# A feed-forward on 256 tokens at a time with its outputs turned, inside an attention kernel

## The chip, the cores and the metric

The kernel runs on one core of a Trainium2 chip. The metric is the device time of one execution in microseconds; lower is better. Besides the timed runs there is one execution taken with the hardware profiler, from which every duration below comes.

## The reference

Four sequences of 2048 tokens with 512 features go through one attention layer with 16 heads of 32 features and one linear layer with weights of +1 and -1, each followed by a residual addition and a normalization. Everything is float32. The essential part is:

```python
q = (x @ Wq.T), k = (x @ Wk.T), v = (x @ Wv.T)          # each split in 16 heads of 32
attn = softmax(q @ k.T / sqrt(32))                       # per head, over 2048 keys
x = layernorm(x + attn @ v)
w = (weights >= 0) * 2 - 1
y = clip((x @ w.T) * scale + bias, -100, 100)            # scale and bias: one per output feature
out = layernorm(x + y)
```

## The kernel before, in words

**Steps.** The attention of four heads is one group `n`, so there are 16 groups (four batch items, four groups of heads each). A group has 64 steps: four blocks of 512 queries (`qb`), each with 16 chunks of 128 keys (`kc`). The whole kernel is one sequence of 1024 steps (`total`), with a lead-in before step 0 and a tail after step 1023. The order of every engine's instructions is the order in which the Python code emits them; nothing is reordered later.

**What a step does.** `scores` (L323) subtracts a maximum (L327) and multiplies queries and keys (L333) for four heads, into four of the eight PSUM banks; ScalarE takes the exponentials (L340) into a buffer `p` from a pool with five buffers. `max_unit` (L264) computes scores for queries some 20 steps ahead (L275), into four other banks, and takes their maxima: VectorE reads three heads from PSUM (L282), and ScalarE copies the fourth to SBUF (`moved`, L294) for VectorE to reduce later. In each even step `weighted` (L344) multiplies the exponentials of the two steps before with the values (L351), and VectorE adds the result to `oT` (L363). GpSimd adds up the exponentials of each block (L377), one addition of 128 x 2048 values a step, 14 a block; two steps into the next block `denominators` (L400) multiplies these sums with ones (L383).

**What fills the odd steps.** All other work on TensorE is a task with a first and a last step, planned ahead by `plan` (L762): "small" tasks (four transposes of 128 x 128: `transpose_x` L221, `turn` L552, `add_attention` L425, weights L136 and L149) and "big" ones (a piece of a projection, L233: `project_q` and `project_k` with 256 columns and weight 2, called wide here; `project_v` with 128 columns, a value piece; and half a feed-forward tile). An odd step takes one small task and big ones of a total weight of about two. Tasks whose last step has come are taken first; the rest follow a fixed order of preference and, in a second pass, a quota of the weights over a group's 64 steps. Fillers are emitted after the step's maximum matmuls and before `later()`, the reduction of `moved`.

**PSUM banks.** `take` (L83) hands out the bank that a small clock model expects free first; eight banks are taken in each step by scores and maxima alone, and a filler takes a ninth. Who is late with a bank holds a later matmul.

**The feed-forward.** `Finish` (L481) works on 512 tokens: load the attention's result, statistics, normalize (`norm`, L542), then for each 128 tokens `turn` (L548): four transposes, a copy rounded to the one-pass float type on ScalarE (`high`, L557), and the rest `low` on VectorE (L559). `ffn` (L563) multiplies both with the weights: the tokens are the stationary operand and the weights stream, so the outputs are [token, feature]. A call covers 256 output features (`half`), or 512 in the last blocks. VectorE then multiplies by scale (L575), adds bias (L576), clips (L577), each on a tile in PSUM, and adds to the row (L579). `finish` (L611) spreads this over the next batch item's steps, one tile every 13 steps; `finish_last` (L632) and `finish_end` (L659) do it for the last batch item, at its end and in the tail. After it come second statistics, `rstd`, `shift`, `norm` and the stores, issued by SP like all loads.

The planner's choice among big tasks before the change:

```python
elif must:
    can = values[:1] or thirds[:1]
elif k == 1:
    can = values[:1] or thirds[:1] or wide[:1]
elif thirds and values:
    can = thirds[:1] + values[:1]
else:
    can = wide[:1] or values[:2] or thirds[:1]
```

Of the kernel before, what the change touches and what calls it, by code (L numbers as in the profile page):

```python
# [21 lines left out]
def kernel(  # L22
# [13 lines left out]
    P = 128  # L36
# [13 lines left out]
    STEPS = NQB * NT  # L50
    HALF = D // 2
    W = 2 * P
# [6 lines left out]
    xpool = ctx.enter_context(tc.tile_pool(name="xpool", bufs=2))  # L59
    stage = ctx.enter_context(tc.tile_pool(name="stage", bufs=2))  # L60
    mpool = ctx.enter_context(tc.tile_pool(name="mpool", bufs=2))
    cpool = ctx.enter_context(tc.tile_pool(name="cpool", bufs=1))
    dram = ctx.enter_context(tc.tile_pool(name="dram", bufs=1, space=bass.MemoryType.DRAM))
# [3 lines left out]
    vpool = ctx.enter_context(tc.tile_pool(name="vpool", bufs=2))  # L67
    ppool = ctx.enter_context(tc.tile_pool(name="ppool", bufs=5))
    apool = ctx.enter_context(tc.tile_pool(name="apool", bufs=2))
    work = ctx.enter_context(tc.tile_pool(name="work", bufs=2))  # L70
    once = ctx.enter_context(tc.tile_pool(name="once", bufs=1))
# [87 lines left out]

    scale_bc = const.tile([P, D], F32, name="scale_bc")  # L160
    bias_bc = const.tile([P, D], F32, name="bias_bc")

    def load_first():

        first = ppool.tile([P, DC, D], F32, tag="p", name="first_w")
        for i, name in enumerate(("wk", "wq", "wv")):
            xin[name, 0] = first[:, i, :]
        for name in ("wk", "wq"):
            nc.scalar.dma_start(out=xin[name, 0], in_=rows_of[name][ds(0, P), :])
        for g in range(NQB):  # L170
            t = ppool.tile([P, NTQ, D], F32, tag="p", name="first_x")
            for j in range(NTQ):
                xin[0, g, j] = t[:, j, :]
                nc.sync.dma_start(out=t[:, j, :], in_=x[0, ds(g * QB + j * P, P), :])

    def load_rest():
        nc.scalar.dma_start(out=xin["wv", 0], in_=wv[ds(0, P), :])
        raws["ws"] = xpool.tile([P, DC, D], F32, tag="xg", name="raw_ws")
        nc.scalar.dma_start(out=raws["ws"], in_=w_ffn.rearrange("(c p) i -> p c i", p=P))
        nc.sync.dma_start(out=scale_bc, in_=ffn_scale.partition_broadcast(P))  # L180
        nc.sync.dma_start(out=bias_bc, in_=ffn_bias.partition_broadcast(P))

# [295 lines left out]

    shared = []

    class Finish:  # L481
        def __init__(self, b, g):
            self.b, self.g = b, g
            self.mv, self.rs, self.nb, self.nT, self.rows_rs = {}, {}, {}, {}, {}
            self.room = None

# [61 lines left out]
        def turn(self, j):  # L548
            i = take()
            pt = cols_of(i, DC, P)  # L550
            for c in range(DC):
                nc.tensor.transpose(pt[:, c, :], self.row(j)[:, ts(c, P)], ident)  # L552
            runs("full", 0.44)

            high = work.tile([P, DC, P], F32R, tag="high", name="high")
            low = work.tile([P, DC, P], F32R, tag="low", name="low")
            nc.scalar.copy(high, pt)  # L557
            spend("ACT", 0.6, clock["PE"] + 0.2)
            nc.vector.tensor_tensor(low, pt, high, ALU.subtract)  # L559
            give(i, "DVE", 0.7)  # L560
            self.nT[j] = high, low

        def ffn(self, j, half):  # L563
            cols = slice(0, D) if half is None else ts(half, HALF)
            wide = D if half is None else HALF
            i = take()
            py = ps[:, i, :wide]
            for k, part in enumerate(self.nT[j]):
                for c in range(DC):
                    nc.tensor.matmul(  # L570
                        py, lhsT=part[:, c, :], rhs=wT["ws"][:, c, cols],
                        start=(k == c == 0), stop=(k == 1 and c == DC - 1),
                    )
            runs("full", 3.4e-3 * wide)
            nc.vector.tensor_tensor(py, py, scale_bc[:, cols], ALU.mult)  # L575
            nc.vector.tensor_tensor(py, py, bias_bc[:, cols], ALU.add)  # L576
            nc.vector.tensor_scalar(py, py, MAX_VAL, -MAX_VAL, ALU.min, ALU.max)  # L577
            dst = self.row(j)[:, cols]
            nc.vector.tensor_tensor(dst, dst, py, ALU.add)  # L579
            give(i, "DVE", 0.6 + 4.2e-3 * wide)  # L580

# [28 lines left out]

    def finish(b, qb, a, every, w, lag):  # L611
        f = Finish(b, qb)
        at(a, f.load)
        for j in range(NTQ):
            at(a + 2 + j, f.stats, 1, j)
        at(a + 6, f.rstd, 1)
        at(a + 7 + lag, f.shift, 1)
        for j in range(NTQ):
            t = a + 8 + lag + every * j
            at(t, f.norm, 1, j)  # L620
            turned = task("small", t + 1, t + 3, f.turn, j)
            for k in range(2):
                task("big", t + 2, t + w, f.ffn, j, k, after=turned)
            at(t + w, f.stats, 2, j)
        e = a + 9 + lag + every * (NTQ - 1) + w
        at(e, f.rstd, 2)
        at(e + 1 + lag, f.shift, 2)
        for j in range(NTQ):
            at(e + 2 + lag + j, f.norm, 2, j)
        at(e + 5 + lag, f.store)  # L630

    def finish_last(qb, last):  # L632
# [8 lines left out]
        at(a + 4, f.shift, 1)  # L641
        for j in range(NTQ):
            t = a + 5 + (j if late else 3 * j)
            by = t + 6
            at(t, f.norm, 1, j)
            if late:
                by = total + (-1, 1, 4, 5)[j]
            turned = task("small", t + 1, t + 3, f.turn, j)
            for k in [None] if late else range(2):
                task("big", by if late else t + 2, by, f.ffn, j, k, after=turned)  # L650
            at(by + late, f.stats, 2, j)
        e = total + 7 if late else a + 21
        at(e, f.rstd, 2)
# [5 lines left out]
    def finish_end(qb, last):  # L659
# [3 lines left out]
        for j in range(NTQ + 1):  # L663
# [3 lines left out]
            if j:  # L667
                at(total + 3, f.shift, 1, j - 1, j)
                at(total + 3, f.norm, 1, j - 1)
        for j in range(NTQ):  # L670
            t = total + (6, 6, 7, 8)[j]
            turned = task("small", t, t, f.turn, j)
            t = total + 7 + j
            task("big", t, t, f.ffn, j, None, after=turned)
            at(t, f.stats, 2, j)
            at(t, f.rstd, 2, j, j + 1)
            at(t + 1, f.shift, 2, j, j + 1)
            at(t + 1, f.norm, 2, j)
            at(t + 1, f.store_tile, j)

# [5 lines left out]
    task("small", -9, -7, transpose_weight, "wv", 0)  # L686
    for _ in range(2):
        at(-8, load_next)
# [7 lines left out]
    for n in range(N):  # L696
# [32 lines left out]
        for qb in range(NQB):  # L729
# [12 lines left out]
            if g == NG - 1:  # L742
                if b < B - 1:
                    every = 13 if b < B - 2 else 11
                    finish(b, qb, (b + 1) * NG * STEPS + qb * (5 * every - 1), every, every, 3)
                else:
                    (finish_end if is_last(n, qb) else finish_last)(qb, last)
# [7 lines left out]

    def on_vector(t):
        return t[3].__name__ == "ffn"

    def weight(t):
        return 2 if t[3] in (project_k, project_q) else 1  # L760

    def plan(quota=None):  # L762
# [9 lines left out]
        while any(len(gone[kind]) < len(tasks[kind]) for kind in tasks):  # L772
# [10 lines left out]
            for kind in most:  # L783
# [8 lines left out]
                if kind == "big":  # L792
                    if middle and quota is not None and not heavy:
                        k = max(1, min(k, -(-quota[group] * (at_n + 1) // STEPS) - used[group]))


                    thirds = [t for t in can if on_vector(t)]
                    values = [t for t in can if t[3] is project_v]
                    wide = [t for t in can if weight(t) == 2]
                    if heavy or any(map(on_vector, must)):  # L800
                        thirds = []
                    k -= sum(map(weight, must))
                    if k < 1:
                        can = []
                    elif must:
                        can = values[:1] or thirds[:1]
                    elif k == 1:
                        can = values[:1] or thirds[:1] or wide[:1]
                    elif thirds and values:
                        can = thirds[:1] + values[:1]  # L810
                    else:
                        can = wide[:1] or values[:2] or thirds[:1]
                else:
                    can = can[: max(0, k - len(must))]
                picked = must + can
                for t in sorted(picked, key=lambda t: not on_vector(t)):
                    gone[kind].add(t[2])
# [93 lines left out]
```

## Time and profile before

| what | us |
|---|---|
| median of 3 runs | 4385.39 (4384.27 to 4385.4) |
| the profiled execution, its own time | 4384.56 |
| its span | 4382.7 |
| TensorE busy, granted clock 0.996 | 4331.6 |
| GpSimd busy | 4083.0 |
| VectorE busy | 3381.3 |
| ScalarE busy | 2994.6 |

A row of the groups names the line, engine, operation, what is written and read, the shapes and the count; then the busy time of all, the mean of one in ns, and the idle time of the engine before them with what ended it. A row of the timeline has the start, the length and then the same names; PE is TensorE's matmuls, PEld its weight loads, DVE is VectorE, ACT ScalarE, POOL GpSimd. A float32 matmul stands as two instructions, as it takes two passes. A matmul that waits for a bank is listed as long, not as idle, so TensorE's busy time contains waits. A row of the waits gives the total, the number and the longest.

### The profile page before, as it was taken

The numbers are of one execution on the slowest core, as the hardware profiler recorded it, in microseconds if no ns is written. First come the engines' busy times: TensorE is split into PE (matmuls) and PEld (weight loads), VectorE is DVE, ScalarE is ACT, GpSimd is POOL, SyncE is SP. The second block draws the span as 40 slices with busy tenths as digits, with TensorE's granted clock in tenths as the row PEclk, the third lists the DMA queues.
The fourth block names the chain that finished last, engine by engine and source line by source line (L and its number), as shares of the span: only waits on it lengthen the run. The fifth ranks groups of instructions, "written<-read, shape, count | busy, mean of one in ns | idle before, by whom it ended". The sixth has DMA issues, their size and how long they took to land.

```text
span 4382.7 us, 88304 instructions
## 1 busy us (share of the span) xinstructions
PE 4331.6 (99%) x35644; PEld 2081.3 (47%) x35644; DVE 3381.3 (77%) x5924; ACT 2994.6 (68%) x6173; POOL 4083.0 (93%) x937
## 2 busy tenths in 40 slices
PE   9999999999999999999999999999999999999997
PEld 5444444444444444445444444444544444444443
DVE  6777777777778777777777877877787777878785
ACT  4666666676667667676676766767666676767675
POOL 4999999999999999999999999999999999999993
PEclk9999999999999999999999999999999999999998
DMA  2000000010001000011000100001100000001101
GB/s 74 11 14 17 11 21 10 16 40 17 21 13 29 11 23 20 11 45 36 21 20 11 33 10 21 23 10 49 28 20 21 20 21 23 20 11 33 24 23 49
DMA packets 259938, 101.60 MB, mean 23 GB/s; under 512 B 168908, under 2 KB 234444, under 8 KB 259528
## 3 DMA queue, kind: packets, MB, share of 16 engines
q1 hardware_dynamic: 258568, 94.12, 8.7%
q8 instruction: 279, 4.57, 0.4%
q10 hardware_dynamic: 960, 1.84, 0.1%
q14 instruction: 131, 1.07, 0.1%
HBM read 54.52 MB, written 33.02 MB: 20 GB/s over the span
## 4 chain that ended last, share of the span: by engine, by line
PE 94%; DVE 2%; POOL 2%; ACT 2%; issue 0%; DMA 0%; ACTq 0%; POOLq 0%; DVEq 0%; SPq 0%
PE ps L275 21%; PE ps L351 21%; PE ps L333 19%; PE ps L233 16%; PE ps L327 8%; PE ps L383 3%; PE ps L570 3%; POOL acc L377 2%; ACT p L340 1%; PE ps L425 1%; PE ps L221 1%; PE ps L552 1%; DVE part L282 1%; DVE st L516 0%; DVE ps L576 0%
## 5 line engine op out<-in xcount | busy, mean ns | idle before, releaser
L377 POOL TENSOR_TENSOR acc<-acc,p 128x2048 f32<-128x2048 f32 x825 | 3744.2, 4538 | 104.1 <-ACT p L340 43.8
L340 ACT ACTIVATE p<-ps 128x512 f32<-128x512 f32 x4096 | 2115.0, 602 | 1148.4 <-PE ps L333 1143.4
L282 DVE TENSOR_REDUCE part<-ps 128x1 f32<-128x512 f32 x3072 | 1933.4, 683 | 660.4 <-PE ps L275 659.8
L275 PE MATMUL ps<-kT,qT 32*128 32x512 f32 x8192 | 1190.5, 592 | 1.9 <-ACT p L340 1.5
L333 PE MATMUL ps<-qT,kT 32*128 32x512 f32 x8192 | 1083.6, 593 | 0.0
L351 PE MATMUL ps<-p,vv 128*32 128x512 f32 x8192 | 984.9, 598 | 1.6 <-DVE low L559 1.0
L275 PEld LDWEIGHTS ps<-kT,qT 32*128 32x128 f32 x8192 | 568.2, 184 | 429.8 <-issue 206.5
L282 DVE TENSOR_REDUCE part<-moved 128x1 f32<-128x512 f32 x1024 | 692.5, 676 | 0.3 <-ACT moved L294 0.3
L294 ACT COPY moved<-ps 128x512 f32<-128x512 f32 x1024 | 631.2, 616 | 20.4 <-PE ps L275 19.7
L351 PEld LDWEIGHTS ps<-p,vv 128*32 128x32 f32 x8192 | 220.3, 109 | 687.4 <-issue 338.4
L327 PE MATMUL ps<-negm,ones_bf 32*128 32x512 bf16 x4096 | 458.2, 384 | 11.6 <-DMA negm<-split 3.9
L333 PEld LDWEIGHTS ps<-qT,kT 32*128 32x128 f32 x8192 | 406.2, 184 | 53.5 <-issue 37.5
L363 DVE TENSOR_TENSOR oT<-ps,oT 128x512 f32<-128x512 f32 x448 | 309.8, 692 | 123.1 <-PE ps L351 81.6
L377 POOL TENSOR_TENSOR acc<-p 128x2048 f32<-128x2048 f32 x64 | 291.0, 4546 | 108.7 <-ACT p L340 108.6
L327 PEld LDWEIGHTS <-ones_bf 32*128 32x128 bf16 x4096 | 106.4, 91 | 558.2 <-issue 521.3
L233 PEld LDWEIGHTS ps<-wvT,xT 128*128 128x128 f32 x2048 | 247.7, 191 | 102.0 <-ACT p L340 96.1
L233 PE MATMUL ps<-wvT,xT 128*128 128x128 f32 x2048 | 283.2, 282 | 0.3 <-ACT p L340 0.3
L233 PE MATMUL ps<-xT,wqT 128*128 128x256 f32 x1024 | 250.6, 388 | 0.0
L233 PE MATMUL ps<-xT,wkT 128*128 128x256 f32 x1024 | 247.2, 387 | 0.2 <-ACT p L340 0.2
L233 PEld LDWEIGHTS ps<-xT,wqT 128*128 128x128 f32 x1024 | 184.1, 189 | 69.2 <-ACT p L340 48.6
L233 PEld LDWEIGHTS ps<-xT,wkT 128*128 128x128 f32 x1024 | 185.3, 190 | 61.3 <-ACT p L340 38.9
L361 DVE COPY oT<-ps 128x512 f32<-128x512 f32 x64 | 44.3, 692 | 131.4 <-PE ps L351 131.4
(76 smaller groups left out, 1755.4 us busy)
## 6 DMA issues: line engine op xcount, KB each, us to landing
xc<-in_L_attn_x_dram SPq DMA_DIRECT2D x60, 256.0 KB
res<-xc SPq DMA_DIRECT2D x60, 256.0 KB
xs<-in_L_attn_x_dram SPq DMA_DIRECT2D x48, 256.0 KB
xg<-res SPq DMA_DIRECT2D x12, 1024.0 KB
out_dram<-xg SPq DMA_DIRECT2D x12, 1024.0 KB
first_x<-in_L_attn_x_dram SPq DMA_DIRECT2D x16, 256.0 KB
xg_last<-res SPq DMA_DIRECT2D x4, 768.0 KB
out_dram<-xg_last SPq DMA_DIRECT2D x3, 1024.0 KB
```

The source lines that it names most:

```text
L233: nc.tensor.matmul(pp, lhsT=lhs(c), rhs=rhs(c), start=(c == 0), stop=(c == DC - 1))
L275: nc.tensor.matmul(ps[:, banks[h], :], lhsT=qT[n, qb][rows, ts(qc, P)], rhs=kT[n][rows, ts(kb, QB)], start=True, stop=True,)
L282: nc.vector.tensor_reduce(part[:, qc, h : h + 1, kb], src, AX.X, ALU.max, negate=True)
L294: nc.scalar.copy(moved, ps[:, banks[-1], :])
L327: nc.tensor.matmul(ps[:, banks[h], :], lhsT=ones_bf[rows, :], rhs=negm[n, qb][rows, :], start=True, stop=False,)
L333: nc.tensor.matmul(ps[:, banks[h], :], lhsT=kT[n][rows, ts(kc, P)], rhs=qT[n, qb][rows, :], start=False, stop=True,)
L340: nc.scalar.activation(p[:, h, :], ps[:, banks[h], :], AF.Exp, scale=SM_SCALE)
L351: nc.tensor.matmul(pb[cols, :], lhsT=vv[n][:, kc, cols], rhs=p[:, h, :], start=(i == 0), stop=(i == 1),)
L363: nc.vector.tensor_tensor(outs[n, qb], pb, outs[n, qb], ALU.add)
L377: nc.gpsimd.tensor_tensor(a, before if kc == 1 else a, p, ALU.add)
L383: nc.tensor.matmul(ps[h * HD : (h + 1) * HD, b, :], lhsT=ones, rhs=p[:, h, :], start=start, stop=stop,)
L570: nc.tensor.matmul(py, lhsT=part[:, c, :], rhs=wT["ws"][:, c, cols], start=(k == c == 0), stop=(k == 1 and c == DC - 1),)
```

## The change

Two tiles of 128 tokens are worked on together as a pair. `turn` writes its `high` and `low` into one half of tiles 256 tokens wide. `ffn` makes the weights the stationary operand and streams the 256 tokens, so the outputs are [feature, token]; a call covers two groups of 128 features, 16 matmuls into one bank. Because a feature is now a partition, scale and bias are one value a partition: ScalarE applies both in one activation for each 128 features, and VectorE clips both into `yT`. A new small task `turn_out` turns 128 tokens back with four transposes, and VectorE adds them to the row.

The planner gives a call of `ffn` weight 2; the former preference for feed-forward beside values is gone. The odd step takes one value piece where a small task is there (`light`) or the quota is not behind, and otherwise a wide task or two value pieces. `finish` has a pair every 26 steps, one block of 512 tokens in each group of 64 steps (22 and 54 in the third batch item). The pools change: `p` 5 to 4 buffers, `work` (`high`, `low`, new `yT`) 2 to 1, `stage` 2 to 3 with one more load in flight, `cpool` 1 to 2. The last blocks and the tail are planned anew in pairs.

```diff
-    stage = ctx.enter_context(tc.tile_pool(name="stage", bufs=2))
+    stage = ctx.enter_context(tc.tile_pool(name="stage", bufs=3))
...
-    cpool = ctx.enter_context(tc.tile_pool(name="cpool", bufs=1))
+    cpool = ctx.enter_context(tc.tile_pool(name="cpool", bufs=2))
...
-    ppool = ctx.enter_context(tc.tile_pool(name="ppool", bufs=5))
+    ppool = ctx.enter_context(tc.tile_pool(name="ppool", bufs=4))
...
-    work = ctx.enter_context(tc.tile_pool(name="work", bufs=2))
+    work = ctx.enter_context(tc.tile_pool(name="work", bufs=1))
...
-        nc.sync.dma_start(out=scale_bc, in_=ffn_scale.partition_broadcast(P))
-        nc.sync.dma_start(out=bias_bc, in_=ffn_bias.partition_broadcast(P))
+        nc.sync.dma_start(out=scale_t, in_=ffn_scale.rearrange("(c p) -> p c", p=P))
+        nc.sync.dma_start(out=bias_t, in_=ffn_bias.rearrange("(c p) -> p c", p=P))
...
-            high = work.tile([P, DC, P], F32R, tag="high", name="high")
-            low = work.tile([P, DC, P], F32R, tag="low", name="low")
+            if j % 2 == 0:
+                self.parts = [
+                    work.tile([P, DC, 2 * P], F32R, tag=part, name=part) for part in ("high", "low")
+                ]
+            high, low = (part[:, :, ts(j % 2, P)] for part in self.parts)
...
-        def ffn(self, j, half):
...
+        def ffn(self, pair, half):
+
+            if half == 0:
+                self.yT = work.tile([P, DC, 2 * P], F32, tag="yT", name="yT")
             i = take()
...
-            nc.vector.tensor_tensor(py, py, scale_bc[:, cols], ALU.mult)
-            nc.vector.tensor_tensor(py, py, bias_bc[:, cols], ALU.add)
-            nc.vector.tensor_scalar(py, py, MAX_VAL, -MAX_VAL, ALU.min, ALU.max)
-            dst = self.row(j)[:, cols]
-            nc.vector.tensor_tensor(dst, dst, py, ALU.add)
-            give(i, "DVE", 0.6 + 4.2e-3 * wide)
+            py = cols_of(i, 2, 2 * P)
+            for f in range(2):
+                for k, part in enumerate(self.parts):
+                    for c in range(DC):
+                        nc.tensor.matmul(
+                            py[:, f, :], lhsT=wT["ws"][:, c, ts(2 * half + f, P)],
+                            rhs=part[:, c, :],
+                            start=(k == c == 0), stop=(k == 1 and c == DC - 1),
+                        )
+            runs("full", 1.9)
+            for f in range(2):
+                oc = slice(2 * half + f, 2 * half + f + 1)
+                nc.scalar.activation(
+                    py[:, f, :], py[:, f, :], AF.Identity,
+                    bias=bias_t[:, oc], scale=scale_t[:, oc],
+                )
+            spend("ACT", 0.75, clock["PE"] + 0.2)
+            nc.vector.tensor_scalar(
+                self.yT[:, 2 * half : 2 * half + 2, :], py, MAX_VAL, -MAX_VAL, ALU.min, ALU.max
+            )
+            give(i, "DVE", 0.7)
+
+        def turn_out(self, j):
+
+            i = take()
+            pt = cols_of(i, DC, P)
+            for c in range(DC):
+                nc.tensor.transpose(pt[:, c, :], self.yT[:, c, ts(j % 2, P)], ident)
+            runs("full", 0.44)
+            nc.vector.tensor_tensor(self.row(j), self.row(j), ps[:, i, :], ALU.add)
+            give(i, "DVE", 0.7)
...
+    def pair(f, i, turn, ffn, back):
+
+        for k in range(2):
+            t = task("small", *turn[k], f.turn, 2 * i + k, after=halves[0])
+        for k in range(2):
+            t = task("big", *ffn[k], f.ffn, i, k, after=t)
+        halves[0] = t
+        for k in range(2):
+            task("small", *back[k], f.turn_out, 2 * i + k, after=t)
+            at(back[k][1] + 1, f.stats, 2, 2 * i + k)
...
+        for i in range(2):
+            t = a + 11 + every * i
+            at(t, f.norm, 1, 2 * i)
+            at(t + 2, f.norm, 1, 2 * i + 1)
+            z = t + every
+            pair(f, i, [(t + 1, t + 5), (t + 3, t + 7)], [(t + 4, z - 10), (t + 4, z - 8)],
+                 [(t + 6, z - 4), (t + 6, z - 2)])
...
-                    every = 13 if b < B - 2 else 11
-                    finish(b, qb, (b + 1) * NG * STEPS + qb * (5 * every - 1), every, every, 3)
+                    every, apart = (26, STEPS) if b < B - 2 else (22, 54)
+                    finish(b, qb, (b + 1) * NG * STEPS + qb * apart, every)
...
-        return 2 if t[3] in (project_k, project_q) else 1
+        return 2 if t[3] in (project_k, project_q) or t[3].__name__ == "ffn" else 1
...
+                    due = quota[group] * (at_n + 1) / STEPS - used[group] if quota else 2
...
+                    light = steps[s] and values and not heavy and due < 2.5
                     if k < 1:
                         can = []
...
+                    elif must or k == 1:
+                        can = values[:1] or ([] if must else wide[:1])
+                    elif light or due < 1.25 and not heavy:
+                        can = values[:1] or wide[:1]
                     else:
-                        can = wide[:1] or values[:2] or thirds[:1]
+                        can = wide[:1] or values[:2]
```

## The prediction

> **What bounds the kernel now.** I read the busy shares first, then the chain of work that ended last, the groups by line, the waits, and last the timeline.
>
> ```profile
> PE 4331.6 (99%) x35644; PEld 2081.3 (47%) x35644; DVE 3381.3 (77%) x5924; ACT 2994.6 (68%) x6173; POOL 4083.0 (93%) x937
> PE 94%; DVE 2%; POOL 2%; ACT 2%; issue 0%; DMA 0%; ACTq 0%; POOLq 0%; DVEq 0%; SPq 0%
> ```
>
> TensorE holds 94% of the chain, so time is what TensorE's instructions take plus the places where it waits. GpSimd is close behind: a block of 16 steps has 14 additions (L377) of 4.54 us that follow each other every 4.61 us, 64.6 us, and some blocks last 64.0 us.
>
> A busy TensorE hides its waits, because a held matmul counts as busy. So I cut the timeline at the first L327 matmul of each step and sorted the steps by the tasks the planner put into the odd one. The odd step with half a feed-forward tile (L570) and a value piece (L233) shows the method:
>
> ```profile
> 1190.04 0.40 PE L327 MATMUL ps<-negm,ones_bf 32*128 32x512 bf16 x4
> ...
> 1194.12 0.39 PE L327 MATMUL ps<-negm,ones_bf 32*128 32x512 bf16 x4
> ...
> 1195.20 1.76 PE L275 MATMUL ps<-kT,qT 32*128 32x512 f32 x8
> ...
> 1195.37 0.42 DVE L579 TENSOR_TENSOR xg<-xg,ps 128x256 f32<-128x256 f32 x1
> ...
> 1195.85 0.29 PEld L275 LDWEIGHTS ps<-kT,qT 32*128 32x128 f32 x2 [0.45 <-DVE xg L579]
> ...
> 1196.90 0.16 PEld L351 LDWEIGHTS ps<-p,vv 128*32 128x32 f32 x8 [0.76 <-ACT p L340]
> ...
> 1198.75 0.10 PEld L327 LDWEIGHTS <-ones_bf 32*128 32x128 bf16 x4 [0.84 <-issue]
> ```
>
> The odd step lasts 4.08 us and the even one 4.63, where an unheld even step lasts 3.90: the fourth head of the next maximum (L275) waits for the bank that VectorE frees after its four operations, 1.67 us into the even step. The wait is 0.73, so a bank that is free 0.94 us into the step costs nothing. The list of waits has this row 63 times:
>
> ```profile
> PEld ps L275 <- DVE xg L579: 28.3, 63, 0.5
> ```
>
> Mean length of an odd step and its even one (without denominators), same method: nothing 6.99; v (a value piece) 7.33; turn v 8.04 (the bank waits for ScalarE's `high`, then VectorE's `low`); wide (a q or k piece) 8.07; v v 8.05; x-transpose v 7.49; half alone 8.24; turn wide 8.30; half v 8.72; half wide 9.12; wide wide 9.59.
>
> **The change, part by part.** VectorE loses 112 x (423+433+433+420) ns and 8 x 2.77 us, 214 us, and gets 64 clips of 0.70 and 64 additions of 0.69, 89 us. By itself that is worth nothing, since VectorE doesn't set the end; it pays only through the banks. TensorE gets 64 x 4 transposes of 0.49 us a group (L552 to L233), 31 us; the matmuls of the feed-forward stay 32 of 256 columns a pair of tiles. ScalarE gets 128 activations.
>
> What those cost is the disputed number. The nearest rows:
>
> ```profile
> L237 ACT COPY qT<-ps 128x256 f32<-128x256 f32 x128 | 47.7, 373 | 49.8 <-PE ps L233 47.3
> L535 ACT ACTIVATE nb<-mv,neg 128x1 f32<-128x1 f32 x128 | 27.9, 284 | 1.2
> L531 ACT ACTIVATE neg<-rs 128x1 f32<-128x1 f32 x8 | 1.5, 193 | 0.2 <-POOL rs L524 0.2
> L542 ACT ACTIVATE xg<-xg,nb,rs 128x512 f32<-128x512 f32 x96 | 80.8, 841 | 0.0
> L577 DVE TENSOR_SCALAR ps<-ps 128x256 f32<-128x256 f32 x112 | 48.5, 433 | 3.9
> L577 DVE TENSOR_SCALAR ps<-ps 128x512 f32<-128x512 f32 x8 | 5.6, 700 | 0.3
> ```
>
> A plain 256-column copy takes 373 ns. But the new activation reads scale and bias from a column each. The trace has 193 ns for one column with a number as scale and 284 with a column, and 841 for 512 columns with two, against 616 for the copy L294. The Trainium skill, ScalarE: Activation LUTs, section What ACT_TABLE_LOAD costs, agrees and speaks against the change: each such operand adds about 93 ns to 186 + 0.833 a column, 585 ns here as an estimate. I take 373 + 2 x 93 = 0.56 us, ends 0.37 and 0.62.
>
> Both halves of a pair's 16 matmuls fill one bank; the built program posts once after all 16, and the second activation waits for the first. So from the next step's start: TensorE's result at +0.10 (the copy after a wide piece starts there, next rows), two activations 1.12 with 0.08 of hand-overs, the clip 0.70: bank free at +2.0.
>
> ```profile
> 1203.16 0.10 PEld L327 LDWEIGHTS <-ones_bf 32*128 32x128 bf16 x4 [0.33 <-issue]
> 1203.26 0.37 ACT L237 COPY qT<-ps 128x256 f32<-128x256 f32 x1 [0.63 <-PE ps L233]
> ```
>
> In the built program the fourth L275 head of the next step is again the one behind it: a wait of 2.0 - 0.94 = 1.06. The odd step is 0.226+0.858+0.957 for scores and maximum and 2.1 to 2.2 for 16 matmuls (16 x 0.131), 4.14. The pair lasts 4.14 + 3.90 + 1.06 = 9.10. With the copy's row it would be 8.73, with ends rounded outward 8.7 and 9.3. VectorE, held by the clip, starts its maxima late and still ends inside the step; ScalarE is through at +1.3, where its exponentials start anyway. For `turn_out` beside a value piece I take x-transpose v, 7.50 (VectorE's addition is done at +0.35), ends 7.47 and, if it behaves as turn v, 8.04; beside a wide piece 8.30.
>
> The order of both built programs, from the planner's new rule, gives the exchange in 64 steps. In six of the eleven groups with a feed-forward in the middle: gone are 6 v, 6 half v, 2 turn wide, wide wide, half wide and half: 43.98 + 52.32 + 16.60 + 9.59 + 9.12 + 8.24 = 139.9. New are 4 double halves, 4 v v, 3 wide, 2 turn v, 2 out v, 2 out wide: 36.4 + 32.2 + 24.2 + 16.1 + 15.0 + 16.6 = 140.5. So +0.6 a group. The 31 us of transposes are nearly paid by fewer held steps. With the other five by the same table: **+4**, ends -14 (8.73) and +25 (9.3 and 8.04).
>
> Four `p` buffers for five: the exponential of step s now needs the addition of step s-4. I laid additions 4.61 apart beside the steps. At five the least lead is about 1 us in steps 80 to 220, and the denominators (L383) wait 3.7 us there in total. At four the lead falls to -3.4 at worst: 5.7 us are lost on the exponentials, and the denominators' waits go. **+2**, ends 0 and +6. Later the least lead is 2.2 us, in blocks of 66 us.
>
> Steps 960 to 1023 have no projections. From 961 to 976 I get 68.3 against 66.5 (two double halves), 65.0 against 68.3 for the next 16 (three empty odd steps); from 993 to 1008, 70.1 now, GpSimd's 64.6 is the floor. That would be -7; late waits are poorly known: **-5**, ends -10 and +3.
>
> The tail, from the last attention addition (L468, 4343.8) to the end, is 38.9 us, nearly all VectorE at four operations of 0.7 a tile. In pairs, ScalarE's order sets it: last normalization at 7.5; four activations of the pair before, 9.8; `high` twice, `low`, 11.8; two halves, 15.5; activations, clip, turn, additions, 20.0; second pair's `high`, `low`, halves, 25; but the first pair's nine last ScalarE instructions stand ahead of its last two activations, 30.1; clip, turn, additions, statistics, 35.1; normalizations 40.5; store 5.5: 46. **+7**, ends +2 and +13, the upper for a TensorE clock that is 0.77 in that window already.
>
> Queues: SP issues two small loads for two broadcasts, one more `xs` load ahead and `xc` into a second buffer; stores move but follow their normalization. No such DMA stands among the waits; the `negm` transposes behind them have 5 steps of cover. Nothing, and 4 us if one came late (the longest such wait was 4.7). `high`, `low` and `yT` have one buffer; the next pair's turn is planned after the last half, so nothing in the middle; in the tail it is counted.
>
> The sum is made on the profiled execution, 4384.56 (span 4382.7): +4 +2 -5 +7 = +8, 4392.6; the median of the runs is 0.8 above it: **4393**.
>
> **Rivals.** Faster: activations at the copy's 0.37, and fewer v steps leaving less lateness to the wide ones (they range from 7.87 to 8.2). Double halves at 8.73 give -13 instead of +4, 4376, and less lateness a few us more: about 4371. For it: many fewer held steps; against it: the two-column rows.
>
> Slower, one mechanism: the bank behind the double half. If it is free at +2.5 rather than +2.0 (half alone is already held 1.15), 52 such pairs cost 26 more: 4419. The point at which it decides is +2.02, where 4394.2 is passed: very near. For it: three operations on two engines in series where a copy was one; against it: VectorE is idle when the clip comes.
>
> GpSimd as the bound through the fourth buffer: only where blocks come under 64.6 us or the lead of 2.2 us is used up; one us in each of 44 blocks would give 4437. The blocks of 66 us speak against it.
>
> **How the numbers follow.** No change can be told within 0.2%, 4376.6 to 4394.2. As summed, 0.42 (0.33 inside that band, 0.09 above it, since 4393 lies near its edge); held bank 0.26; GpSimd or a longer tail 0.10; faster 0.22, of it 0.02 inside. Together: faster 0.20, same 0.33 + 0.02, slower 0.09 + 0.26 + 0.10. Range: the sum's ends that are likely together, 4370 to 4420, leave out the GpSimd case and the deepest gain.
>
> **What would show it.** The new activations' mean (0.56), double-half pairs at 9.1, a wait of L275 on the clip about 50 times, out v at 7.5, L340 waiting for L377 only in steps 80 to 260, a tail of 46 us. Wrong would be: waits of the exponentials on L377 in every block, or activations near 0.37.

## The result and the profile after

The changed kernel takes 4414.75 us (median of 5 runs, 4414.12 to 4416.56), the kernel before beside it 4385.4 (4384.27 to 4387.53): ratio 1.0067, 95% interval 1.0056 to 1.0078. It is slower by 29 us. The prediction was 4393 with a range of 4370 to 4420: the range holds it, but the likeliest case was 22 us too low.

First the busy shares and the chain of work that ended last, of the kernel after:

```profile
PE 4345.3 (98%) x35964; PEld 2089.9 (47%) x35964; DVE 3262.4 (74%) x5572; ACT 3057.9 (69%) x6301; POOL 4083.7 (93%) x937
PE 90%; POOL 6%; DVE 2%; ACT 1%; issue 1%; DMA 0%; ACTq 0%; POOLq 0%; DVEq 0%; SPq 0%
```

VectorE lost 119 us, and the kernel is slower all the same. TensorE is listed 13.7 us busier: transposes were added, and held matmuls count as busy. GpSimd's share of the chain went from 2 to 6%; a part of it is shown further down.

The two profiled executions (4382.7 and 4412.3 us of span), cut at the same places as in the prediction, in us:

| stretch | before | after | difference | predicted |
|---|---|---|---|---|
| start to step 256 (fewer `p` buffers) | 1109.1 | 1110.8 | +1.7 | +2 |
| steps 256 to 959 (the feed-forward) | 2954.5 | 2970.8 | +16.3 | +4 |
| step 960 to the last attention addition | 280.2 | 283.5 | +3.3 | -5 |
| tail behind it | 38.9 | 47.3 | +8.4 | +7 |

So two terms were right and two were not: 12 us are missing in the middle and 8 near the end.

**The pair that the prediction worked out.** The timeline of a double half and the even step behind it, after (engine, line, instruction, tiles; in brackets the idle time before it and what ended it):

```profile
1304.58 0.39 PE L326 MATMUL ps<-negm,ones_bf 32*128 32x512 bf16 x4
...
1304.74 1.11 ACT L579 ACTIVATE ps<-ps,bias_t,scale_t 128x256 f32<-128x256 f32 x2 [0.43 <-PE ps L571]
...
1305.89 0.69 DVE L584 TENSOR_SCALAR yT<-ps 128x512 f32<-128x512 f32 x1 [1.44 <-ACT ps L579]
1305.92 2.06 ACT L339 ACTIVATE p<-ps 128x512 f32<-128x512 f32 x4
...
1306.63 0.29 PEld L274 LDWEIGHTS ps<-kT,qT 32*128 32x128 f32 x2 [0.77 <-DVE yT L584]
...
1309.54 0.40 PE L326 MATMUL ps<-negm,ones_bf 32*128 32x512 bf16 x4
```

The even step starts at 1304.58; the activations start 0.16 later, take 1.11 together, the clip ends at 1306.58. The bank is free 2.00 us into the step, and the fourth head of the maximum goes on then. The even step lasts 4.96 where an unheld one lasts 3.90: a wait of 1.06. The pair's mean over 41 is 9.11. The groups and the waits, after:

```profile
L579 ACT ACTIVATE ps<-ps,bias_t,scale_t 128x256 f32<-128x256 f32 x128 | 68.8, 538 | 33.9 <-PE ps L571 31.4
L584 DVE TENSOR_SCALAR yT<-ps 128x512 f32<-128x512 f32 x64 | 44.2, 691 | 113.8 <-ACT ps L579 113.8
L594 PE MATMUL ps<-ident,yT 128*128 128x128 f32 x256 | 43.1, 291 | 12.1 <-DVE yT L584 11.9 <-ACT p L339 0.2
```

```profile
ACT ve L519 <- DVE mv L514: 42.0, 19, 5.4
PEld ps L274 <- DVE yT L584: 38.7, 50, 0.8
ACT p L339 <- POOL acc L376: 20.4, 13, 2.5
```

The wait on the clip stands there 50 times, 0.77 us each. It takes the place of the 63 waits on the old addition. The first row is the one that I hadn't foreseen. Before, the same wait was this:

```profile
ACT ve L522 <- DVE mv L517: 26.8, 11, 6.1
```

Between steps 256 and 959 it stood there once before, with 0.9 us; now it stands there 11 times, with 2.35 to 3.34 us each.

**The wait that was missed.** The timeline after around the last statistics of a block of 512 tokens, in a step with one value piece (L513 and L514 are the statistics, L519 adds epsilon for the reciprocal deviation, `rstd`):

```profile
1646.78 0.68 DVE L513 BATCH_NORM_STATS2 st<-xg 128x6 f32<-128x512 f32 x1
1647.49 0.18 DVE L514 BATCH_NORM_AGGREGATE mv<-st 128x2 f32<-128x6 f32 x1
...
1647.71 0.30 ACT L519 ACTIVATE ve<-mv,eps_t 128x4 f32<-128x4 f32 x1 [2.36 <-DVE mv L514]
1647.91 2.04 ACT L339 ACTIVATE p<-ps 128x512 f32<-128x512 f32 x4
1648.54 0.97 PEld L232 LDWEIGHTS ps<-wvT,xT 128*128 128x128 f32 x8 [1.89 <-ACT p L339]
```

`pair` puts the statistics of the last row one step behind its `turn_out`, at z-1, and `finish` puts `rstd` at z-1 too. ScalarE reaches L519 before VectorE has done the statistics, waits 2.36 us, and its exponentials stand behind. They free TensorE's banks late: the value piece starts 1.89 us late, where an undisturbed one starts 0.76 late. Such a v pair lasts 8.51 us, not 7.33.

### The profile page after: what moved, and what is told of

Its sections match the earlier page's. It is cut to its first block, busy times and chain, and to the rows that moved or that the text cites. A ratio compares the mean times of both kernels' runs of the same rounds, so it can differ in the third digit from the quotient of the medians.

```text
span 4412.3 us, 88749 instructions
## 1 busy us (share of the span) xinstructions
PE 4345.3 (98%) x35964; PEld 2089.9 (47%) x35964; DVE 3262.4 (74%) x5572; ACT 3057.9 (69%) x6301; POOL 4083.7 (93%) x937
## 4 chain that ended last, share of the span: by engine, by line
PE 90%; POOL 6%; DVE 2%; ACT 1%; issue 1%; DMA 0%; ACTq 0%; POOLq 0%; DVEq 0%; SPq 0%
PE ps L274 21%; PE ps L350 20%; PE ps L332 18%; PE ps L232 15%; PE ps L326 7%; POOL acc L376 6%; PE ps L382 3%; PE ps L571 3%; DVE part L281 1%; ACT p L339 1%; PE ps L220 1%; PE ps L424 1%; PE ps L594 1%; PE ps L549 1%; DVE st L513 0%
## 5 line engine op out<-in xcount | busy, mean ns | idle before, releaser
L281 DVE TENSOR_REDUCE part<-ps 128x1 f32<-128x512 f32 x3072 | 1932.9, 683 | 695.8 <-PE ps L274 694.0
L332 PE MATMUL ps<-qT,kT 32*128 32x512 f32 x8192 | 1071.3, 591 | 0.0
L274 PEld LDWEIGHTS ps<-kT,qT 32*128 32x128 f32 x8192 | 553.0, 185 | 446.8 <-issue 242.4
L281 DVE TENSOR_REDUCE part<-moved 128x1 f32<-128x512 f32 x1024 | 692.4, 676 | 14.2 <-ACT moved L293 14.2
L326 PE MATMUL ps<-negm,ones_bf 32*128 32x512 bf16 x4096 | 438.8, 384 | 12.8 <-ACT p L339 4.2
```

The source lines that it names most:

```text
L274: nc.tensor.matmul(ps[:, banks[h], :], lhsT=qT[n, qb][rows, ts(qc, P)], rhs=kT[n][rows, ts(kb, QB)], start=True, stop=True,)
L281: nc.vector.tensor_reduce(part[:, qc, h : h + 1, kb], src, AX.X, ALU.max, negate=True)
L326: nc.tensor.matmul(ps[:, banks[h], :], lhsT=ones_bf[rows, :], rhs=negm[n, qb][rows, :], start=True, stop=False,)
L332: nc.tensor.matmul(ps[:, banks[h], :], lhsT=kT[n][rows, ts(kc, P)], rhs=qT[n, qb][rows, :], start=False, stop=True,)
```

## The experiments

The differences between experiments below are of medians, those of a stretch of profiled executions. All but the one on the kernel before are edits of the changed kernel.

### Reciprocal deviation later

```diff
-        at(z - 1, f.rstd, 2)
+        at(z + 1, f.rstd, 2)
```

> The changed kernel with one edit: in the middle of the kernel the second reciprocal deviations (rstd) stand two steps later, not in the step of the last statistics. Theory: ScalarE's small activation there waits 2.4 us for VectorE's statistics and holds the exponentials, 1.18 us a time, 11 or 12 times: 13 to 14 us less, 4401. Rival (that wait is hidden, and the loss lies in the bank behind the double halves alone): unchanged, 4413 to 4416.

Measured: 4404.74 (4401.05 to 4406.02), ratio to before 1.0038 (1.0023 to 1.0053), 10 us less than the changed kernel. v pairs fell from 7.89 on the mean to 7.34. In one of the groups with 22 steps a pair instead of 26, however (steps 832 to 895), 3.5 us were lost. The waits of this experiment have the reason, a row that the changed kernel has once and with 2.8 us:

```profile
ACT neg L528 <- POOL rs L521: 8.7, 3, 3.4
```

`shift` (L528) stands at z+3, two steps behind this `rstd`. The power is computed on GpSimd, where it queues between additions of 4.5 us, and two steps were too few twice. The longest of these waits, 3.4 us, is in step 881, in the group that lost; soon behind it the granted TensorE clock is 0.5 for 3.4 us. One step later instead of two should have the gain without this loss:

```diff
-        at(z - 1, f.rstd, 2)
+        at(z, f.rstd, 2)
```

> The changed kernel with the reciprocal deviation of the second normalization one step behind the last statistics, and not two as in the earlier run of this kind, which gained 10 us in all but lost 3.5 us in the group with the longer spacing. Theory (only the wait in the same step costs; the loss in that group came of the second step's delay): 11 v pairs at 7.3 instead of 8.51 are -13, none lost, so 4401 to 4402. Rival (the loss in that group is the price of any delay): 4404 to 4406. Rival (one step is not enough for VectorE to get there, so the wait stays): 4411 or above.

Measured: 4399.06 (4397.08 to 4399.81), ratio 1.0029 (1.0018 to 1.0041), 15.7 less than the changed kernel. The row of the missed wait, here:

```profile
ACT ve L519 <- DVE mv L514: 11.1, 9, 5.4
```

The group that lost 3.5 us now gains 1.1, and steps 256 to 959 take 2958.4, 12.4 less. That is +3.9 against before, where the prediction has +4. The theory stands: one line that puts two tasks into the same step is 12.4 of the 16.3 us of the middle. Another 2.2 went from the stretch behind step 960, where step 985 had the same wait (4.95 to 2.48).

### Numbers instead of columns

```diff
-                    bias=bias_t[:, oc], scale=scale_t[:, oc],
+                    scale=1.25,
```

This leaves the scale and bias of each feature out.

> The changed kernel with scale as a number (1.25) and no bias in the new activations; the real scale and bias are left out of the computation. Theory: an activation falls from 0.54 to about 0.37, the bank behind a double half is free 0.33 us sooner, the wait of 1.06 falls to 0.73 in some 46 pairs: 15 us less, 4400. Rival (the activations lie beside other work, and something else holds the step): unchanged within 3 us.

Measured: 4395.19, ratio 1.0021 (1.0013 to 1.0028), 19.6 less.

```profile
L579 ACT ACTIVATE ps<-ps 128x256 f32<-128x256 f32 x128 | 47.1, 368 | 35.0 <-PE ps L571 32.6
```

538 ns became 368, the copy's price; each column operand costs 85. The double half went from 9.11 to 8.76, by 0.35, what two activations lost (0.34): the time is on the path in full. 41 pairs by 0.35 are 14.4 of the 15.8 us that the middle lost. What of the 19.6 lies outside the middle (0.5 at the start, 1.9 behind step 960, 1.4 in the tail) wasn't followed.

### Five `p` buffers again, and four in the kernel before

```diff
-    stage = ctx.enter_context(tc.tile_pool(name="stage", bufs=3))
+    stage = ctx.enter_context(tc.tile_pool(name="stage", bufs=2))
...
-    cpool = ctx.enter_context(tc.tile_pool(name="cpool", bufs=2))
+    cpool = ctx.enter_context(tc.tile_pool(name="cpool", bufs=1))
...
-    ppool = ctx.enter_context(tc.tile_pool(name="ppool", bufs=4))
+    ppool = ctx.enter_context(tc.tile_pool(name="ppool", bufs=5))
...
-    for _ in range(3):
+    for _ in range(2):
```

> The changed kernel with five buffers for p again, and two for the x loads and one for xc as before. Theory: the fifth buffer matters only in steps 80 to 260, where waits on the exponentials are exchanged for waits of the denominators: 2 to 3 us less, 4412. Rival (GpSimd, 6% of the chain instead of 2%, is what was lost): 15 us less or more, 4400.

Measured: 4411.59, ratio 1.0055 (1.004 to 1.007), 3.2 less; the start is 1108.9, about what it was before. And the kernel before with one buffer less, its first weights laid into the pool of the sums:

```diff
-    ppool = ctx.enter_context(tc.tile_pool(name="ppool", bufs=5))
+    ppool = ctx.enter_context(tc.tile_pool(name="ppool", bufs=4))
...
-        first = ppool.tile([P, DC, D], F32, tag="p", name="first_w")
+        first = apool.tile([P, DC, D], F32, tag="acc", name="first_w")
```

> The kernel before with one edit: four buffers for p instead of five (the first weights then lie in the pool of the sums, as in the change). Theory: 2 to 3 us more, 4388, all of it in steps 64 to 260. Rival (the fourth buffer costs in every block): 15 us more or above.

Measured: 4388.0, ratio 1.0004 (0.9995 to 1.0013), so about 2 us, which its interval doesn't tell from none. Both directions, 3.2 and about 2, are near the +2 of the prediction, the second not clear of noise, and the rival of GpSimd as the bound in every block through the fourth buffer is out.

### The clip away from the bank

If the activation writes to SBUF, the bank is free 0.7 us earlier, before the clip:

```diff
-                    py[:, f, :], py[:, f, :], AF.Identity,
+                    self.yT[:, 2 * half + f, :], py[:, f, :], AF.Identity,
...
-            nc.vector.tensor_scalar(
-                self.yT[:, 2 * half : 2 * half + 2, :], py, MAX_VAL, -MAX_VAL, ALU.min, ALU.max
-            )
-            give(i, "DVE", 0.7)
+            give(i, "ACT", 1.1)
+            y = self.yT[:, 2 * half : 2 * half + 2, :]
+            nc.vector.tensor_scalar(y, y, MAX_VAL, -MAX_VAL, ALU.min, ALU.max)
+            spend("DVE", 0.7, clock["ACT"])
```

> The changed kernel with the new activations writing to yT in SBUF, and the clip done there in place, so that the bank is free after ScalarE. Theory: free at +1.3 instead of +2.0, the wait behind a double half falls from 1.06 to 0.35 in some 46 pairs: 32 us less, 4383, near the kernel before. Rival (VectorE's place in its own queue, not the bank, holds the step): the clip still stands before VectorE's maxima, so less than 8 us.

Measured: 4471.27, ratio 1.0191 (1.0176 to 1.0206), 56 us more. A miss in sign. The clip's row in this experiment:

```profile
L585 DVE TENSOR_SCALAR yT<-yT 128x512 f32<-128x512 f32 x64 | 147.5, 2305 | 117.1 <-ACT yT L579 117.1
```

The same clip takes 2305 ns instead of 691, now that it reads SBUF. The timeline of this experiment shows two clips, each with GpSimd's additions around it:

```profile
1191.91 13.84 POOL L376 TENSOR_TENSOR acc<-acc,p 128x2048 f32<-128x2048 f32 x3
...
1196.99 4.39 DVE L585 TENSOR_SCALAR yT<-yT 128x512 f32<-128x512 f32 x1 [1.28 <-ACT yT L579]
```

```profile
1321.51 4.55 POOL L376 TENSOR_TENSOR acc<-acc,p 128x2048 f32<-128x2048 f32 x1
1325.92 1.02 ACT L579 ACTIVATE yT<-ps,bias_t,scale_t 128x256 f32<-128x256 f32 x2 [3.07 <-PE ps L571]
1326.98 0.43 DVE L585 TENSOR_SCALAR yT<-yT 128x512 f32<-128x512 f32 x1 [4.04 <-ACT yT L579]
```

The second clip starts after an addition has ended (1326.06) and before the next (1333.40): 0.43 us. The first starts at 1196.99, while one of the additions runs; this one ends at 1201.09 and the clip at 1201.37, 0.28 later. So it is with all 64: the 50 clips that start while an addition runs end 0.28 to 0.29 us after that addition, and the 14 others take 0.39 to 0.43. So the clip waits for the end of the addition that runs. The Trainium skill (SBUF — State Buffer, section SBUF: two separate sides) says so: VectorE and GpSimd share a pair of ports that is locked for a whole instruction, against VectorE operations in a two-port mode or with two inputs in SBUF; and VectorE: DVE Perf Modes, section Why PSUM operands drop a tier, has a PSUM operand rule that mode out. The trace agrees with both: 0.43 alone in SBUF, and 0.66 to 0.69 from PSUM beside the same additions. Not every read of SBUF waits: the maximum of `moved` (L281, 128 x 512 from SBUF) took 0.69 at most, 1024 times in this experiment. I had carried the PSUM price over to SBUF, beside an engine that adds 93% of the time.

Two more things are in this trace. The even step behind nearly every double half is 0.88 shorter than in the changed kernel, so the bank did come free sooner. And between steps 256 and 959 the granted TensorE clock is 0.5 in nine stretches of 3.4 or 6.8 us, 51 us together, where the changed kernel has none. At half clock half of that time is lost at most, so up to 26 of the 56 us are the clock's, as an estimate; what lets it fall was not tested.

With the activation still writing to SBUF, but the clip behind the turn back, in PSUM before the addition, the lock is out of play:

```diff
-            nc.vector.tensor_tensor(self.row(j), self.row(j), ps[:, i, :], ALU.add)
-            give(i, "DVE", 0.7)
+            y = ps[:, i, :]
+            nc.vector.tensor_scalar(y, y, MAX_VAL, -MAX_VAL, ALU.min, ALU.max)
+            nc.vector.tensor_tensor(self.row(j), self.row(j), y, ALU.add)
+            give(i, "DVE", 1.4)
```

> The changed kernel; the new activations write to yT in SBUF, and the clip is done in turn_out, on PSUM, ahead of the addition. Theory (the bank behind the double half; and the clip on SBUF was slow because VectorE and GpSimd share a way to SBUF, as GpSimd adds all the time): the clip takes 0.70 again, the bank is free at +1.3, a double-half pair lasts 8.4: 28 to 32 us less, 4385. Rival (the clip on SBUF was slow because of its operand's shape, or the bank isn't what holds the step): no gain, 4405 or more.

Measured: 4395.93, ratio 1.0022 (1.0014 to 1.0031), 19 less; the clip is back at 690 ns, from PSUM. The size was missed: the clip's time came off one bank and went to the bank of `turn_out`. The double half fell from 9.11 to 8.25, but out v (`turn_out` beside a value piece) rose from 7.58 to 8.47 and out wide from 8.49 to 8.70.

### A bank for each 128 features

To the edit above: each group of 128 features takes a bank of its own, and its activation starts after its own eight matmuls.

```diff
-            i = take()
-            py = cols_of(i, 2, 2 * P)
             for f in range(2):
+                i = take()
+                py = ps[:, i, : 2 * P]
...
-            runs("full", 1.9)
-            for f in range(2):
+                runs("full", 1.05)
                 oc = slice(2 * half + f, 2 * half + f + 1)
                 nc.scalar.activation(
-                    py[:, f, :], py[:, f, :], AF.Identity,
+                    self.yT[:, 2 * half + f, :], py, AF.Identity,
```

> As e6_clip_later, and each of a call's two groups of 128 features has its own bank and its own activation, which starts when its 8 matmuls are done. Theory: the second bank is free at about +1.0, just in time: double-half pairs last 8.1, some 44 us less than the change, 4371, below the kernel before. Rival (a tenth bank in a step makes another matmul wait): no better than e6_clip_later, 4385.

Measured: 4385.2 (4383.18 to 4385.9), ratio 0.9998 (0.9989 to 1.0007): level with the kernel before, 29.6 less than the changed one. The double half fell to 8.06, its wait of 1.06 gone. Out v (8.46) and out wide (8.70) stay as in the last experiment. Against the changed kernel, 41 x 1.05 less and 13 x 0.88 + 18 x 0.21 more is 28 less; the middle lost 24.4, and the difference wasn't followed.

### The first pair's end in the tail

The reciprocal deviation, shift, normalization and store of the first pair of the tail come one step later, so that ScalarE does the second pair's activations before them; the `rstd` of the block before it one step later too.

```diff
-        at(e, f.rstd, 2)
+        at(e + late, f.rstd, 2)
...
+            u = t + 4 + (i == 0)
             for j in (2 * i, 2 * i + 1):
-                at(t + 4, f.rstd, 2, j, j + 1)
+                at(u, f.rstd, 2, j, j + 1)
             for j in (2 * i, 2 * i + 1):
-                at(t + 4, f.shift, 2, j, j + 1)
-                at(t + 4, f.norm, 2, j)
-                at(t + 4, f.store_tile, j)
+                at(u, f.shift, 2, j, j + 1)
+                at(u, f.norm, 2, j)
+                at(u, f.store_tile, j)
```

> The changed kernel; in the tail the first pair's last statistics, normalizations and stores stand one step later, behind the second pair's activations, and the last reciprocal deviation of the third quarter stands one step later. Theory: ScalarE's nine small instructions no longer hold the second pair: 4 to 6 us less, 4410, all in the tail. Rival (the tail's length is the chain of the second pair itself): within 1 us.

Measured: 4413.37, ratio 1.0061 (1.0045 to 1.0078), 1.4 less, not clear of noise. The tail itself went from 47.3 to 44.5. But step 986, where this kernel's instructions are the changed kernel's, took 8.64 us in its profiled execution instead of 5.75; with five buffers it took 6.92. Here is this step in the changed kernel, with five buffers and in this experiment; a row has the window, its length, the busy time of each engine (PE, PEld, DVE, ACT, POOL), and as the third number from its end the granted TensorE clock:

```profile
4193.58:4199.33 5.75, 5.63 (x38) 1.69 (x35) 2.81 (x5) 4.89 (x13) 5.75 (x4) 1.00 0.00 0
4192.02:4198.94 6.92, 6.80 (x39) 2.50 (x37) 2.80 (x5) 4.96 (x13) 6.92 (x4) 0.75 0.00 0
4193.56:4202.20 8.64, 8.52 (x40) 2.24 (x38) 2.80 (x5) 5.00 (x13) 8.56 (x5) 0.60 0.00 0
```

So the step is longer by the clock, and not in this experiment alone; in the profiled execution its 2.9 us hide the 2.8 of the tail. What I named for the tail is worth at most 2.8 of its 8.4 us, less than the 4 to 6 expected. What makes up the rest stays open.

### Without single values beside turns

```diff
-                    light = steps[s] and values and not heavy and due < 2.5
+                    light = False
```

> The changed kernel without its rule that single values go beside turns (light is always False); nothing is left out of the computation. In steps 256 to 959 the order changes so: wide value projections alone 90 to 62, v 17 to 48, turn with v 37 to 20, turn with wide 8 to 25, out with v 22 to 10, out with wide 21 to 32. Theory (a step's price is that of its kind): turn v 8.06 and wide 7.98 are 16.04 us, turn wide 8.30 to 8.49 and v 7.33 are 15.63 to 15.82, so each of 13 to 17 exchanges gives back 0.2 to 0.4; out v 7.58 and wide 7.98 are 15.56, out wide 8.49 and v 7.33 are 15.82, so each of 11 costs 0.26. Sum -6 to +1, taken -3: about 4412, and the middle part 1 to 5 us shorter. Rival (single values beside turns is where the 16 us of the middle went): -12 or more, 4403 or below. Rival (the rule helps, because turns beside wide projections have no room): +5 or more, 4420 or above.

Measured: 4413.16, ratio 1.0062 (1.0047 to 1.0077), 1.6 less, not clear of noise; the middle 2.9 less (2967.9). That is small, as the prices of the pairs say; the rule is not where the time went.

### The losses mended together

> The two-bank form (a bank and an activation for each 128 features, clip behind the turn back) with the reciprocal deviation of the last rows one step behind their statistics instead of in the same step, and five p buffers (stage 2, constants 1). Theory (the three losses are separate and add): two banks 4385, the moved deviation 10 less, the fifth buffer 3 less: 4372, with the last v pair of a group back at 7.3 to 7.5. Rival (they share one cover, so that the second and third give nothing once the first is mended): 4383 to 4386.

Measured: 4367.51 (4365.65 to 4367.81), ratio 0.9958 (0.9941 to 0.9975). v pairs are at 7.33. That is 17.7 below the two-bank version, where the theory added up 13. On the profiled executions it is 19.9: 12.1 in the middle, 1.8 at the start, 4.0 behind step 960 and 2.0 in the tail. On the changed kernel the moved `rstd` alone gave 15.7 and the fifth buffer 3.2, 18.9 together. So the losses add; none hid behind another.

> The mended version, and besides it without the rule that single values go beside turns. Theory (a step's price is that of its kind): with clip and addition out v is 8.46 and out wide 8.70, so an exchange of out v and wide (16.44) for out wide and v (16.03) gives back 0.4 on 11 pairs, and the turns 0.2 to 0.4 on 13 to 17: 7 to 11 less than the mended version, about 4363. Rival (wide steps with a turn or an output keep banks so long that the neighbours wait): the same as the mended version or slower.

Measured: 4355.28 (4354.1 to 4357.27), ratio 0.993 (0.9916 to 0.9945), 31 us faster than the kernel before. Busy shares and chain of this last version:

```profile
PE 4306.3 (99%) x35964; PEld 2088.8 (48%) x35964; DVE 3264.3 (75%) x5572; ACT 3050.8 (70%) x6301; POOL 4083.9 (94%) x937
PE 91%; POOL 5%; ACT 1%; DVE 1%; issue 1%; DMA 0%; ACTq 0%; POOLq 0%; SPq 0%; DVEq 0%
```

TensorE has the same 35964 matmuls as in the changed kernel and is busy 39 us less: that much of its busy time was no work, but matmuls held or run at a lower clock. The edit that gave 1.6 on the changed kernel gives 12.2 here (by the medians; 0.1 and 8.3 by the profiled executions). In the changed kernel an exchange of out v and wide (7.58 + 7.98) for out wide and v (8.40 + 7.34, without the missed wait) costs 0.18; with two VectorE operations behind the turn it is 8.46 + 7.96 for 8.56 + 7.34, and gives 0.52. Eleven of these would make 7.7 us of the difference between the two gains; that is reckoned from the pairs, not tested alone.

## Why the prediction was right or wrong

**Double half, 9.10: right**, 9.11, for its own reasons. The activation is 538 ns, where 560 was taken; the start is at +0.16 instead of +0.10; the bank is free at +2.00 as said. The rival of activations at the copy's price falls, and so does the rival of the bank at +2.5. With numbers the pair came down by 0.35 where the prediction's ends differ by 0.37. The Trainium skill's price for a column operand (ScalarE: Activation LUTs, section What ACT_TABLE_LOAD costs) was the better guide than the copy's row alone, though its 93 ns each were 85 here; where each activation has a bank of its own and writes to SBUF, it took 586 ns, and the estimate from that page was 585.

**The exchange of steps, +4: right in the sum of what it counted, wrong as the middle's total**, +16.3. Its failing step is the use of the table of pairs on the new order: "new are 4 double halves, 4 v v, 3 wide, ..." prices a step by what TensorE does in it. The v pair of 7.33 was measured where statistics and `rstd` were apart. In the new order the last statistics and `rstd` of a block fall into one step, and 7.33 became 8.51. With `rstd` one step later the middle is +3.9. Within this the sizes aren't all right: out wide is 8.49 and not 8.30, out v 7.58 and not 7.50, wide 7.98 and not 8.07; they cancel, so that +3.9 comes so near to +4 is in part luck. Luck it is, too, that the range holds the time: its upper end stood for a bank free later than +2.0 and for a longer tail, and the 12.4 us were in no term and no rival.

**Four `p` buffers, +2: right in size.** +1.7 at the start, 3.2 back with five, and about 2 in the kernel before, not clear of noise. The prediction said waits of exponentials only in steps 80 to 260; 12.0 of the 20.4 us in the list are there, and 5.8 are in steps 1008 and 1010, near the end, where it saw none.

**Steps 960 to 1023, -5: wrong**, +3.3. By stretches, before and after: 961 to 976 66.6 and 68.3, as said. 977 to 992 68.3 and 69.8, where 65.0 was said; 2.3 of it is the missed wait in step 985. 993 to 1008 70.0 and 61.9, lower than the floor of 64.6 that was set; and the last 14 steps, which the prediction left out, 54.3 and 62.7. The chain that ended last, after, shows what happened (its rows of 2.6 us and more; in both rows named issue an addition is running):

```profile
4242.64 4.55 POOL acc L376
4247.26 4.55 POOL acc L376
4251.87 4.54 POOL acc L376
4256.48 4.55 POOL acc L376
4261.10 2.61 POOL acc L376
4267.78 3.40 issue
4271.22 4.56 POOL acc L376
4275.86 4.55 POOL acc L376
4280.49 4.55 POOL acc L376
4285.12 4.52 POOL acc L376
4289.72 9.03 POOL acc L376 x2
4298.82 4.59 POOL acc L376
4304.75 3.35 issue
4308.13 4.54 POOL acc L376
4318.07 3.57 PE ps L350 x16
```

From 4242 to 4313 GpSimd's additions set the end. TensorE ran ahead of them through the third block and waited for them in the fourth. Two steps carry that: 1010 (4.76 before, 9.54 after), where exponentials wait 2.53 and 2.06 us for a buffer that an addition still reads, and 1016 (3.04 and 8.87), where `shift` waits 2.83 us for a power behind the additions and exponentials stand behind it. The granted clock is then 0.5 for 3.4 and 6.8 us. With five buffers step 1010 is no shorter (11.69): the denominators wait there, 4.01 us, for an addition. The prediction had the right floor and applied it to one block; in this chain it goes on into the next, and what the third block gained (8.1) the fourth gave back (8.4). This is read off the traces and not tested by a run of its own. That the two blocks together were as long before (124.3, after 124.6) is not GpSimd's doing: between 4203 and 4330 that chain has no addition.

**Tail, +7 to 46: the size right**, 47.3. Of the cause it named, ScalarE's nine instructions ahead of two activations, at most 2.8 us were shown; so the size is in part luck. A lower clock is not the cause: it is 0.68 in the tail before and 0.73 after. The prediction's 0.77 is of the stretch from 4328 on, not of the tail.

**Queues: right.** The waits on transfers are those of before: 4.8 and 3.9 us on `negm` (4.7 and 3.9 before), and the first weights at the start.

## What to carry to other kernels

A table of measured steps prices a new order only as long as every engine's instructions in such a step are those it was measured with: go through each step that gained or lost a small task, and look whether a producer and its consumer on another engine have fallen into one step in front of work that others need. A bank's time is what to lower here, not an engine's: with 119 us less on VectorE the kernel was slower, while a bank for each 128 features gave 29.6 us with the clip moved, and one line of order 15.7. A consumer must also be kept far enough behind a producer that sits in another engine's long queue: here two steps behind GpSimd were too few twice, and with three neither of these waits was left. Before a longer step is put down to an edit, its granted clock is to be read: the same instructions took 5.75 us at 1.00 and 8.64 at 0.60.

## What the hardware showed unexpectedly

A VectorE clip of 128 x 512 float32 values takes 0.69 us from PSUM, 0.43 in SBUF while GpSimd does not add, and up to 4.46 us in SBUF while GpSimd adds, until 0.28 us after the running addition has ended; 2.3 on the mean of all. An operation with one tensor from SBUF and one from PSUM (L596, 678 ns, 680 at most) isn't slowed, nor is a maximum over 512 values in SBUF (L281, 676 ns).

The granted TensorE clock falls to 0.5 for 3.4 or 6.8 us at a time even where the mean of the execution is 0.995: in step 986 not at all in some, for 3.4 us in others and for 6.8 in one, which made 5.75, 6.92 and 8.64 us of the same instructions.
